# Mixture-of-experts stage on TensorE: the products with w1 and w3 run over a number of slot columns chosen per expert at run time

## The chip, the cores and the metric

The kernel runs on one core of a Trainium2 chip. The metric is the device time of one execution in microseconds. The kernel before took 5398.9 us (median of three runs, 5396.42 to 5399.67). All matrix products are in 32-bit floating point.

## The reference

Eight sequences of 512 tokens with 512 features each pass through three blocks, each followed by a residual sum and a layernorm: a Mamba block (state-space scan), a cross-attention block with 16 heads, and a mixture-of-experts block. Only the last one is touched by the change; cut to what matters it is

```
logits = x @ wg.T;  scores = softmax(logits)            # 4096 tokens, 32 experts
keep the 4 best of 8 groups, then the 4 best experts (K = 4); weights normalised over the 4
cap = int(1.25 * 4096 * 4 / 32)                         # 640 slots per expert
each (token, expert) pair takes the next free slot of that expert; pairs beyond 640 are dropped
xe  = tokens gathered by slot                           # 32 x 640 x 512, empty slots are zero
h   = silu(xe @ w1[e]) * (xe @ w3[e])                   # 512 x 512 weights per expert
out = (h @ w2[e]) * weight of the slot
y[token] += out;   plus a shared expert silu(x @ sw1) * (x @ sw3) @ sw2
```

Counted with the reference's own gate on its own inputs, the 32 experts receive between 316 and 750 pairs; 16025 of the 16384 pairs fit into the slots. One expert has at most 320 pairs, five have 321 to 384, six 385 to 448, five 449 to 512, six 513 to 576, and nine have more than 576.

## The kernel before

`layers` (line 89) computes Mamba, attention, the gate and the shared expert, interleaved by a hand-written order; it also writes each token's row, its weights and its number into a DRAM buffer `xbuf` that has 640 rows per expert. `experts` (line 1225 on) then walks the 32 experts in order, and `finish` (line 1472) does the last layernorm. A scheduler of the framework orders instructions within a stretch of straight code; the source order is its starting point, and each engine runs its own list strictly in order, with semaphore waits between engines.

For one expert `e`, `load(e + 1)` (line 1245) issues on SP's queue the next expert's token rows `xe` (L1250, 1362.5 KB) and its three weights `w` (L1253, 1024 KB each). `xe` has two buffers, so the load for expert e + 1 can only start when expert e - 1 no longer needs its own rows; their last readers are the five scatters of that expert (L1394), which take the row numbers from `xe`. `flip` (line 1279) transposes `xe` on TensorE, one slot tile of 128 rows at a time (five tiles, `CJ`), and DVE copies the result to `xT` (L1286). `sums_x` (line 1288) forms the sums that a Strassen-Winograd product needs: all 512x512 products are done as seven half-size products instead of eight, with the slots cut into two halves of 320 (`HALF`).

`hidden` (line 1319) is called twice per expert (r = 0, 1) and issues the seven products, each once for w1 and once for w3. `product` (line 1311) is two matmuls of 320 columns; each of them shows as two records in the profile. That makes 14 groups of eight records (one product for w1 and w3) per expert. ACT copies partial results out of PSUM (`keep`, L1328) and applies silu (L1341); DVE adds and multiplies (`use`, L1335 and L1339) into `hT`. The generator `side` lets DVE form weight sums for the next expert in between. `give` (line 1375) does the product with w2 for slot tiles 0 to 3 as seven half-size products of 256 columns, and slot tile 4 (the fifth, `j = CJ - 1`) as four plain matmuls of 512 columns (L1416, tile `po`), then scatters the five tiles of `y` with an accumulating indirect DMA on GpSimd (`put`, L1394). Between its steps it calls `between` (line 1447), which issues the five flips of the next expert.

All matmuls of all experts run at full width: 640 slots, filled or not. An empty slot holds zeros and a weight of zero.

## Time and profile before

| | |
|---|---|
| median of three runs | 5398.9 us |
| the profiled execution | 5406.3 us, of which the span of its instructions is 5404.6 us |
| TensorE (PE) busy | 4672.4 us, 86% |
| VectorE (DVE) busy | 4235.9 us, 78% |
| ScalarE (ACT) busy | 2593.6 us, 48% |
| one expert (4521.9 to 4569.8 us) | 47.9 us: PE 47.90, DVE 28.42, ACT 13.32, POOL 7.99 us busy |
| instruction fetches of PE (queue q8) | 137 packets of 16 KB |

The span is cut into 40 slices of 135 us. Layers fill the first 27 slices or so, with DVE busiest, and the experts the last 13, with PE busiest. In a group's row, "x" is the number of records and "mean ns" the length of one; matmul records overlap, so the distance between the starts of two runs of matmuls tells more than the mean of one. "PEld" is the loading of weights into the array, which overlaps the matmul before it. An arrow in the list of waits reads "engine, tile and line that waited <- what ended the wait: total, times, longest".

### The profile page before, as it was taken

Reading aid. Unit: us, or ns where it says so; the run is one execution under the profiler, and the core shown is the slowest. Engines: PE = TensorE matmul, PEld = TensorE weight load, DVE = VectorE, ACT = ScalarE, POOL = GpSimd, SP = SyncE. Lnnn points to the kernel's source line nnn. Section 1 sums busy time; section 2 is a strip of 40 time slices with the busy share of each in tenths; the row PEclk is TensorE's granted clock in tenths of the full one; section 3 lists DMA queues with packets and bytes.
Section 4 is the critical chain, followed back from the end, with each engine's and each line's share of the span. In section 5 each row is a group of like instructions: output and inputs, shape, how many; then the busy total and the mean of one; then the engine's idle time right before and its main releaser. Section 6 shows DMA issues by size and latency. Waiting matters only on the chain. (4 is left out here: it accounts for less than half of the span.)

```text
span 5404.6 us, 53991 instructions
## 1 busy us (share of the span) xinstructions
PE 4672.4 (86%) x17320; PEld 2476.6 (46%) x17320; DVE 4235.9 (78%) x5369; ACT 2593.6 (48%) x5726; POOL 570.3 (11%) x426
## 2 busy tenths in 40 slices
PE   6768889788888988988888888789999999999994
PEld 3324234234333423433333342333677777777773
DVE  7999899989989989898998998943566555665554
ACT  5566565565656556566565655523222222222223
POOL 1000002002000200200200020011111111111111
PEclk8879989999999999999999999899999999999997
DMA  8875346345444634634544463342344444544544
GB/s 236 266 224 146 87 96 208 81 114 176 114 104 117 197 77 109 189 98 107 174 125 100 117 200 78 91 146 66 103 128 127 123 117 118 127 127 121 129 115 144
DMA packets 486427, 719.03 MB, mean 133 GB/s; under 512 B 117137, under 2 KB 200625, under 8 KB 484096
## 3 DMA queue, kind: packets, MB, share of 16 engines
q1 hardware_dynamic: 450128, 627.16, 41.1%
q0 software_dynamic: 33280, 76.90, 7.5%
q10 hardware_dynamic: 2736, 11.54, 0.5%
q8 instruction: 137, 2.24, 0.2%
q14 instruction: 146, 1.20, 0.1%
HBM read 391.24 MB, written 165.05 MB: 103 GB/s over the span
## 5 line engine op out<-in xcount | busy, mean ns | idle before, releaser
L480 ACT ACTIVATE l_da<-rep,l_aneg 128x256 f32<-128x256 f32 x2048 | 895.0, 501 | 941.8 <-DVE h L501 877.0
L501 DVE TENSOR_TENSOR_SCAN h<-l_da,h 128x1028 f32<-128x1028 f32 x512 | 1166.0, 2292 | 20.3 <-ACT l_da L480 17.7
L494 DVE TENSOR_TENSOR h<-rep,bc 128x1024 f32<-128x1024 f32 x512 | 614.7, 1218 | 103.1 <-PE py L521 84.6
L510 DVE TENSOR_TENSOR h<-h,bc 128x1024 f32<-128x1024 f32 x512 | 619.5, 1217 | 2.1
L521 PE MATMUL py<-h,l_fold 128*32 128x512 f32 x2048 | 368.3, 644 | 113.4 <-DVE h L510 96.5
L813 PE MATMUL ps_s<-l_ka,l_qa 64*128 64x512 f32 x1024 | 325.6, 707 | 137.8 <-DVE mx L815 137.6
L1314 PE MATMUL ps_h<-xT,w 128*128 128x320 f32 x1536 | 435.8, 433 | 0.0
L1394 POOL DMA_INDIRECT based<-y,xe x160 | 255.5, 1597 | 1309.9 <-ACT y L1417 630.0
L1335 DVE TENSOR_TENSOR hT<-ps_h,p 128x320 f32<-128x320 f32 x128 | 62.9, 492 | 378.5 <-PE ps_h L1314 378.5
L815 DVE TENSOR_REDUCE mx<-ps_s 128x2 f32<-128x1024 f32 x256 | 310.2, 1217 | 58.5 <-PE ps_s L813 58.3
L1314 PEld LDWEIGHTS ps_h<-xT,w 128*128 128x128 f32 x1536 | 292.5, 191 | 118.3 <-issue 0.4
L855 PE MATMUL po<-eT,l_va 128*64 128x512 f32 x1024 | 301.5, 670 | 47.6 <-ACT eT L843 43.1
L839 PE MATMUL ps_t<-l_qa,l_ka 64*128 64x512 f32 x1024 | 308.4, 674 | 23.8 <-ACT eT L843 23.1
L843 ACT ACTIVATE eT<-ps_t 128x1024 f32<-128x1024 f32 x256 | 259.0, 1015 | 128.8 <-PE ps_t L839 128.5
L688 POOL DMA_INDIRECT xbuf<-x2t,dest x128 | 217.2, 1697 | 860.4 <-DVE dest L679 760.8
L1314 PE MATMUL ps_h<-t,s 128*128 128x320 f32 x1024 | 286.1, 432 | 0.0
L343 PE MATMUL ps_z<-xnT,wm 128*128 128x256 f32 x1024 | 238.0, 388 | 30.0 <-DVE o L561 24.3
L750 PE MATMUL ps_p<-x2T,wa 128*128 128x512 f32 x512 | 241.5, 626 | 18.1 <-ACT hT L944 10.4
L552 PE MATMUL po<-wm,zs 128*128 128x512 f32 x512 | 244.7, 632 | 13.8 <-DVE z L957 11.9
L343 PE MATMUL ps_x<-xnT,wm 128*128 128x256 f32 x1024 | 246.5, 393 | 4.5 <-ACT xnT L332 2.5
L343 PEld LDWEIGHTS ps_z<-xnT,wm 128*128 128x128 f32 x1024 | 194.6, 193 | 93.0 <-DVE o L561 37.5
L343 PEld LDWEIGHTS ps_x<-xnT,wm 128*128 128x128 f32 x1024 | 196.1, 195 | 80.5 <-issue 43.8
(232 smaller groups left out, 7170.4 us busy)
## 6 DMA issues: line engine op xcount, KB each, us to landing
w<-in_w SPq DMA_DIRECT2D x93, 1024.0 KB
wm<-in_in_proj_w SPq DMA_DIRECT2D x128, 512.0 KB
rep<-dt SPq DMA_DIRECT2D x256, 256.0 KB
rep<-dtx SPq DMA_DIRECT2D x256, 256.0 KB
xbuf<-zero SPq DMA_DIRECT2D x32, 1362.5 KB
xe<-xbuf SPq DMA_DIRECT2D x32, 1362.5 KB
wm<-in_out_proj_w SPq DMA_DIRECT2D x64, 512.0 KB
wa<-in_sw SPq DMA_DIRECT2D x24, 1024.0 KB
```

The source lines that it names most:

```text
L343: nc.tensor.matmul(ps[:, i, :], w[:, dc, i * P : (i + 1) * P], f["xnT"][:, dc, :], start=(dc == 0), stop=(dc == DC - 1),)
L480: nc.scalar.activation(da[:, n, 1:], dt[:, j, i, :], AF.Exp, scale=aneg[:, 2 * q + i, 2 * jj + j, g : g + 1])
L494: nc.vector.tensor_tensor(h[:, :, 1:], dtx.rearrange("p j i t -> p (j i) t"), f["bc", g][0], ALU.mult)
L501: nc.vector.tensor_tensor_scan(flat, da.rearrange("p n t -> p (n t)"), flat, 0.0, ALU.mult, ALU.add)
L510: nc.vector.tensor_tensor(h[:, :, 0:T], h[:, :, 1:], f["bc", g][1], ALU.mult)
L521: nc.tensor.matmul(f["py"][j * QP : (j + 1) * QP, :, :], fold, hs[j // 2][:, 2 * (j % 2) : 2 * (j % 2) + 2, 0:T], start=False, stop=g == N ...
L813: nc.tensor.matmul(ps[:, j, :], qa[r, lt * P : (lt + 1) * P], ka[r, :], start=True, stop=True)
L815: return lambda: nc.vector.tensor_reduce(mx[:, lt, :].unsqueeze(2), ps, AX.X, ALU.max) and None
L839: nc.tensor.matmul(ps[:, j, :], ka[r, kc * P : (kc + 1) * P], qa[r, :], start=True, stop=True)
L843: nc.scalar.activation(eT, ps, AF.Exp)
L855: nc.tensor.matmul(po[j * 2 * HD : (j + 1) * 2 * HD, :], va[:, kc, i, j * HD : (j + 2) * HD], eT[:, j, :], start=(kc == 0), stop=(kc == SC ...
L1314: nc.tensor.matmul(ps, w[:, n, r * P : (r + 1) * P], x[:, n, :], start=not more and n == 0, stop=n == 1, skip_group_check=more,)
```

## The change

The gate, after the last batch, computes for each expert a number from 0 to 5 into a new SBUF tile `arm`: how many of the thresholds 320, 384, 448, 512, 576 its number of pairs exceeds. It stands for the widths `COLS` = 160, 192, 224, 256, 288, 320 columns per half.

So that empty slots end up at the end of both halves, the halves are now the even and the odd slots: `flip`'s copy reads PSUM with a stride of two, and `use` writes `hT` with a stride of two.

At the start of each expert PE and DVE each load `arm[e]` into a register. Each of the seven steps of `hidden` becomes a `tc.Switch` on PE: six arms, one per width, each with the four matmuls (two of w1, two of w3) at that width; an indirect jump chooses the arm and each arm ends in a jump to the common exit. The other engines see no arms: ACT and DVE still work on all 320 columns, the columns beyond the width being stale. After each `hidden`, a Switch on DVE clears the columns of `hT` beyond the width. In `give`, slot tile 4 is a Switch too: the arms for up to 512 pairs are empty, the other two hold the four matmuls. PSUM tiles are now fixed rings, zeroed once, instead of pool tiles.

In the built program there are per expert 15 such jumps into an arm on PE (14 in `hidden`, one in `give`) and two on DVE. Each switch is a stride constant, two address instructions with the jump, and six arms; each arm begins with a prefetch hint for its own exit. The matmuls listed for PE grow from 9300 to 18388 and the branches from 2 to 2946. The position of the flips moves, too: before, the five flips of the next expert stood in `give`; in the changed program 16 of an expert's 20 transposes stand in the second `hidden`, the first of them after the 11th of its 14 switches.

```diff
+COLS = tuple(range(160, HALF + 1, 32))
+PE, DVE = mybir.EngineType.PE, mybir.EngineType.DVE
...
+        if not clock:
+            many, more = taken[:, SC, :], taken[:, 1, :]
+            nc.vector.tensor_scalar(more, many, float(2 * COLS[0]), None, ALU.is_gt)
+            for c in COLS[1:-1]:
+                to = arm if c == COLS[-2] else more
+                nc.vector.scalar_tensor_tensor(to, many, float(2 * c), more, ALU.is_gt, ALU.add)
...
-    psx = ctx.enter_context(tc.tile_pool(name="e_psx", bufs=3, space=PSUM))
-    psy = ctx.enter_context(tc.tile_pool(name="e_psy", bufs=2, space=PSUM))
+    psh = ctx.enter_context(tc.tile_pool(name="e_psh", bufs=1, space=PSUM))
...
+    def ring(n, width, name):
+        held = [psh.tile([P, width], F32, name=f"{name}{i}") for i in range(n)]
+        for t in held:
+            nc.vector.memset(t, 0.0)
+        return cycle(held)
+
+    xh, yh, oh = ring(3, HALF, "ps_x"), ring(2, HALF, "ps_y"), ring(2, D, "ps_o")
...
-        nc.vector.tensor_copy(got["xT"][:, :, j * P : (j + 1) * P], ps.rearrange("p (c t) -> p c t", c=DC))
+        to = got["xT"].rearrange("p c (k t) -> p c k t", k=2)[:, :, :, j * P // 2 : (j + 1) * P // 2]
+        nc.vector.tensor_copy(to, ps.rearrange("p (c t k) -> p c k t", c=DC, k=2))
...
-                ps, w[:, n, r * P : (r + 1) * P], x[:, n, :], start=not more and n == 0, stop=n == 1,
+                ps[:, 0:cols], w[:, n, r * P : (r + 1) * P], x[:, n, 0:cols], start=not more and n == 0, stop=n == 1,
...
-            to = hT[:, 2 * i + r, k * HALF : (k + 1) * HALF]
+            to = hT.rearrange("p c (t k) -> p c t k", k=2)[:, 2 * i + r, :, k]
...
+        def products(more, *parts):
+
+            for n in tc.Switch({PE: got["arm", PE]}, len(COLS)):
+                for ps, w, t in parts:
+                    product(ps, w, r, t, more, COLS[n])
...
-        for m, (w, s1, s2, s3, s4) in enumerate(ws):
-            product(xs[m], s2, r, t2, more=True)
-            pu.append(keep(xs[m], m, "pu"))
+        products(True, *((xs[m], ws[m][2], t2) for m in both))
+        pu = [keep(xs[m], m, "pu") for m in both]
...
+        for n in tc.Switch({DVE: got["arm", DVE]}, len(COLS)):
+            if COLS[n] < HALF:
+                nc.vector.memset(hT.rearrange("p (i r) t -> p i r t", r=2)[:, :, r, 2 * COLS[n] :], 0.0)
...
-        po = pso.tile([P, D], F32, tag="po", name="po")
-        for ic in range(DC):
-            nc.tensor.matmul(po, hT[:, ic, j * P : (j + 1) * P], w2[:, ic, :], start=(ic == 0), stop=(ic == DC - 1))
+        po = next(oh)
+        for n in tc.Switch({PE: got["arm", PE]}, len(COLS)):
+            for ic in range(DC if 2 * COLS[n] > j * P else 0):
+                nc.tensor.matmul(po, hT[:, ic, j * P : (j + 1) * P], w2[:, ic, :], start=(ic == 0), stop=(ic == DC - 1))
...
+        for engine, queue in ((PE, nc.tensor), (DVE, nc.vector)):
+            got["arm", engine] = queue.value_load(arm[0:1, e : e + 1])
```

More of the change, by code (lines that the diff above doesn't have):

```diff
@@ L1 @@
 from contextlib import ExitStack
-from itertools import chain
+from itertools import chain, cycle
 import concourse.bass as bass
@@ L86, in layernorm, with layers @@
     return wait(roots)
-def layers(ctx, tc, a, x1d, filld, based, xbuf):
+def layers(ctx, tc, a, x1d, filld, based, xbuf, arm):
     nc = tc.nc
@@ L1217, in layers, with experts @@
     dry()
-def experts(ctx, tc, a, xbuf, based):
+def experts(ctx, tc, a, xbuf, based, arm):
     nc = tc.nc
@@ L1235, in experts @@
     p2 = ctx.enter_context(tc.tile_pool(name="e_p2", bufs=2))
-    psx = ctx.enter_context(tc.tile_pool(name="e_psx", bufs=3, space=PSUM))
-    psy = ctx.enter_context(tc.tile_pool(name="e_psy", bufs=2, space=PSUM))
+    psh = ctx.enter_context(tc.tile_pool(name="e_psh", bufs=1, space=PSUM))
     pst = ctx.enter_context(tc.tile_pool(name="e_pst", bufs=1, space=PSUM))
-    pso = ctx.enter_context(tc.tile_pool(name="e_pso", bufs=2, space=PSUM))
+    def ring(n, width, name):
[4 more added lines that the diff above has]
+    xh, yh, oh = ring(3, HALF, "ps_x"), ring(2, HALF, "ps_y"), ring(2, D, "ps_o")
     ident = cp.tile([P, P], F32, name="e_ident")
@@ L1309, in sums_w2, with product @@
             yield
-    def product(ps, w, r, x, more=False):
+    def product(ps, w, r, x, more=False, cols=None):
         for n in range(2):
             nc.tensor.matmul(
-                ps, w[:, n, r * P : (r + 1) * P], x[:, n, :], start=not more and n == 0, stop=n == 1,
+                ps[:, 0:cols], w[:, n, r * P : (r + 1) * P], x[:, n, 0:cols], start=not more and n == 0, stop=n == 1,
                 skip_group_check=more,
@@ L1341, in use @@
                 nc.scalar.activation(to, v, AF.Silu)
-        p1, pu, p5 = [], [], []
-        xs = [None, None]
-        for m, (w, s1, s2, s3, s4) in enumerate(ws):
-            xs[m] = psx.tile([P, HALF], F32, tag="h", name="ps_h")
-            product(xs[m], A(w, 0, 0), r, B(x, 0, 0))
-            p1.append(keep(xs[m], m, "p1"))
-        for m, (w, s1, s2, s3, s4) in enumerate(ws):
-            ps = psy.tile([P, HALF], F32, tag="h2", name="ps_h")
-            product(ps, A(w, 0, 1), r, B(x, 1, 0))
-            use(m, 0, 0, ps, p1[m])
+        def products(more, *parts):
+            for n in tc.Switch({PE: got["arm", PE]}, len(COLS)):
+                for ps, w, t in parts:
+                    product(ps, w, r, t, more, COLS[n])
@@ L1353, in hidden @@
+        xs = [next(xh) for m in both]
+        products(False, *((xs[m], A(ws[m][0], 0, 0), B(x, 0, 0)) for m in both))
+        p1 = [keep(xs[m], m, "p1") for m in both]
+        ys = [next(yh) for m in both]
+        products(False, *((ys[m], A(ws[m][0], 0, 1), B(x, 1, 0)) for m in both))
+        for m in both:
+            use(m, 0, 0, ys[m], p1[m])
         next(side, None)
-        for m, (w, s1, s2, s3, s4) in enumerate(ws):
-            product(xs[m], s2, r, t2, more=True)
-            pu.append(keep(xs[m], m, "pu"))
+        products(True, *((xs[m], ws[m][2], t2) for m in both))
@@ L1357, in hidden @@
+        pu = [keep(xs[m], m, "pu") for m in both]
         next(side, None)
-        ys = []
-        for m, (w, s1, s2, s3, s4) in enumerate(ws):
-            ys.append(psy.tile([P, HALF], F32, tag="h2", name="ps_h"))
-            product(ys[m], s1, r, t1)
-            p5.append(keep(ys[m], m, "p5"))
+        ys = [next(yh) for m in both]
+        products(False, *((ys[m], ws[m][1], t1) for m in both))
+        p5 = [keep(ys[m], m, "p5") for m in both]
         next(side, None)
-        for m, (w, s1, s2, s3, s4) in enumerate(ws):
-            product(xs[m], s3, r, t3, more=True)
+        products(True, *((xs[m], ws[m][3], t3) for m in both))
@@ L1366, in hidden @@
+        for m in both:
             use(m, 1, 1, xs[m], p5[m])
-        for m, (w, s1, s2, s3, s4) in enumerate(ws):
-            product(ys[m], s4, r, B(x, 1, 1), more=True)
+        products(True, *((ys[m], ws[m][4], B(x, 1, 1)) for m in both))
+        for m in both:
             use(m, 0, 1, ys[m], pu[m])
         next(side, None)
-        for m, (w, s1, s2, s3, s4) in enumerate(ws):
-            product(xs[m], A(w, 1, 1), r, t4, more=True)
+        products(True, *((xs[m], A(ws[m][0], 1, 1), t4) for m in both))
@@ L1373, in hidden @@
+        for m in both:
             use(m, 1, 0, xs[m])
+        for n in tc.Switch({DVE: got["arm", DVE]}, len(COLS)):
+            if COLS[n] < HALF:
+                nc.vector.memset(hT.rearrange("p (i r) t -> p i r t", r=2)[:, :, r, 2 * COLS[n] :], 0.0)
     def give(e, got, side):
@@ L1408, in give @@
         for r in both:
-            xs.append(psx.tile([P, HALF], F32, tag="h", name="ps_o")[:, 0:FH])
+            xs.append(next(xh)[:, 0:FH])
             product(xs[r], A(hT, 0, 0), r, BW(w2, 0, 0))
@@ L1420, in give @@
         for r in both:
-            ps = psy.tile([P, HALF], F32, tag="h2", name="ps_o")[:, 0:FH]
+            ps = next(yh)[:, 0:FH]
             product(ps, A(hT, 0, 1), r, BW(w2, 1, 0))
@@ L1429, in give @@
         for r in both:
-            zs.append(psy.tile([P, HALF], F32, tag="h2", name="ps_o")[:, 0:FH])
+            zs.append(next(yh)[:, 0:FH])
             product(zs[r], s1, r, t1)
@@ L1518, in program @@
     nc = tc.nc
-    with tc.tile_pool(name="dram", bufs=1, space=DRAM) as dram:
+    with tc.tile_pool(name="dram", bufs=1, space=DRAM) as dram, tc.tile_pool(name="one", bufs=1) as one:
         x1d = dram.tile([N, D], F32, name="x1d")
@@ L1524, in program @@
         xbuf = dram.tile([SLOTS, ROW], F32, name="xbuf")
+        arm = one.tile([P, E], I32, name="arm")
         nc.scalar.preload_act_table_set(LN_EXP)
         with ExitStack() as ctx:
-            layers(ctx, tc, a, x1d, filld, based, xbuf)
+            layers(ctx, tc, a, x1d, filld, based, xbuf, arm)
         with ExitStack() as ctx:
-            experts(ctx, tc, a, xbuf, based)
+            experts(ctx, tc, a, xbuf, based, arm)
         with ExitStack() as ctx:
```

## The prediction

> **What bounds the kernel now.** I read the page's busy row and slices first, to see which stage the change is in and who is busy there.

> ```profile
> PE 4672.4 (86%) x17320; PEld 2476.6 (46%) x17320; DVE 4235.9 (78%) x5369; ACT 2593.6 (48%) x5726; POOL 570.3 (11%) x426
> ...
> PE   6768889788888988988888888789999999999994
> ...
> DVE  7999899989989989898998998943566555665554
> ...
> PEclk8879989999999999999999999899999999999997
> ...
> q8 instruction: 137, 2.24, 0.2%
> ```

> The last 13 slices are the experts: PE full, DVE about half. Next the windows of one expert, from the first product of its `hidden` to that of the next, and of the tail.

> ```profile
> 4521.90:4569.80 47.90, 47.90 (x198) 35.43 (x197) 28.42 (x52) 13.32 (x29) 7.99 (x5) 1.00 0.49 122
> 5300.00:5404.60 104.60, 34.01 (x133) 24.89 (x131) 41.26 (x137) 36.76 (x70) 9.25 (x6) 0.68 0.53 178
> ```

> PE is busy 47.90 of 47.90 us at a granted clock of 1.00; DVE 28.42. So an expert lasts as long as its matmuls. The timeline of PE gives their price by distance of starts:

> ```profile
> 4499.86 2.32 PE L1314 MATMUL ps_h<-xT,s 128*128 128x320 f32 x8
> 4502.01 2.32 PE L1314 MATMUL ps_h<-t,w 128*128 128x320 f32 x8
> 4504.16 0.60 PE L1285 MATMUL ps_t<-e_ident,xe 128*128 128x128 f32 x4
> 4504.60 1.89 PE L1314 MATMUL ps_o<-w,hT 128*128 128x256 f32 x8
> 4506.33 3.60 PE L1416 MATMUL po<-w,hT 128*128 128x512 f32 x8
> 4509.76 0.60 PE L1285 MATMUL ps_t<-e_ident,xe 128*128 128x128 f32 x4
> ```

> Eight records of 320 columns take 2.15 us, of 256 columns 1.73, of 512 columns 3.43, four of 128 columns 0.44: 0.84 ns per column each. An expert is 14 x 2.15 + 7 x 1.73 + 3.43 + 5 x 0.44 = 47.8 us.

> Last, the scatters and the load that follows them (POOL's timeline, then SP's), because `xe` is loaded only when they are done:

> ```profile
> 4520.16 1.54 POOL L1394 DMA_INDIRECT based<-y,xe  x1 [7.49 <-DVE y L1391]
> 4527.77 1.54 POOL L1394 DMA_INDIRECT based<-y,xe  x1 [6.07 <-DVE hT L1339]
> 4533.32 1.54 POOL L1394 DMA_INDIRECT based<-y,xe  x1 [4.01 <-ACT hT L1341]
> 4538.85 1.54 POOL L1394 DMA_INDIRECT based<-y,xe  x1 [3.98 <-ACT p L1328]
> ```
> ```profile
> 4543.50 0.37 SPq L1250 DMA_DIRECT2D xe<-xbuf  x1
> 4551.14 0.37 SPq L1253 DMA_DIRECT2D w<-in_w  x1
> ```

> The scatters follow each other at 5.5 us; the load starts 4.65 us after the last, and the DMA view of that stretch shows its bytes until 4549.2. That is 27.3 us after this `hidden` began (4521.9); the first transposes come at 4552.0. The slack is 2.8 us.

> **What the change removes.** With the counts per expert, mean width is (160 + 5x192 + 6x224 + 5x256 + 6x288 + 9x320)/32 = 261 columns of 320. `hidden` drops from 30.1 to 24.6 us of matmuls per expert, 177 us over 32. Seventeen experts leave out `po`, 17 x 3.43 = 58 us. Together 236 us of PE, 4.4%, if nothing takes its place. Divided by 480 jumps that is 0.49 us per jump.

> **What it adds on PE's sequencer.** 480 switches, each with a jump in and a jump out. The trace of before has no jump inside the work, so I bound it. Near end: at the start of the program's timeline POOL goes through a branch and starts again 0.29 us later; with code already there a switch is 0.6 us of sequencer time, and PE has 1.76 us of matmuls per switch to hide it. Far end: code that must be fetched. q8 shows how PE gets code: 137 packets of 16 KB for 34,640 records and 611 semaphore instructions, one per 257, the last at 5299.7 us with 270 records to go, so code is fetched about one packet ahead of what runs. Windows of 5 us that hold one such packet give it 1.5% and 1.3% of 16 engines, 1.2 and 1.0 us. The first load of the kernel is issued at 0.81 us and its first bytes appear in the DMA view at 1.9: 1.1 us. So a fetch on demand is 1.1 + 1.2 = 2.3 us; between 1.2 (the packet alone) and 3.75 us (that first load, 0.81 to its user at 4.56).

> Do the arms have to be fetched? Packed together, six arms are some 108 instructions and lie inside the next packet. Against that: the dispatch multiplies an index by a stride constant, and every arm begins with a hint to prefetch its own exit. A hint for a jump of 18 instructions would serve nothing, so I take each arm and each exit to lie in another fetch unit. The jump in has no hint. Then a switch is: fetch of the arm 2.3, waiting first for the packet ahead that the sequencer started on its own (1.2), fetch of the exit 2.3 (hinted, but the arm's instructions are too few to cover it), two jumps 0.6: T = 6.4 us. Bounds: 2 x 1.2 + 0.6 = 3.0 and 2 x 3.75 + 1.2 + 0.6 = 9.3. As T is above the 1.76 us of matmuls, PE runs dry in each.

> [...]

> **The sum per expert.** `hidden`: 14 x 6.4 = 89.6 us; 16 of the 20 transposes lie inside its stalls and add nothing. `give`: seven products 12.1, four transposes 0.4, `po` 3.43 x 15/32 = 1.6, and its jump, of which the group of 1.7 us ahead covers a part: 4.7. Loading `arm` into PE's register has no row: between 0.3 (a jump) and 3.75 (a load), taken 2.0, since the queue is short there. DVE's switch at the end of the second `hidden` stands before `sums_w(got, "hT")` and the first product of `give` reads what it clears: 6.4 plus a clear of up to 640 columns (0.8, from DVE's 128x640 rows), less PE's own exit fetch 2.3 and 0.9 of transposes: 4.0 (1 to 7). In sum 114.4 us against 47.9, +66.5, times 32 = +2128. The profiled execution took 5406.3 us, 7.4 above the median: 5406.3 + 2128 - 7.4 = 7527, said as 7500.

> **Edits costed at nothing, and their cover.** Copies and `use` with stride two: 5 x 0.69 and 12 x 0.49 us per expert; even doubled, DVE has 28.4 + 9.3 of 47.9 us, and more now. ACT still copies full width, 13.3 us. DVE's switch after the first `hidden`, 6.4 us, delays `use` of the next steps, which PE reaches 6.4 us apart. Gate: five small DVE operations (0.17 us each), off the path of the scatters. Seven clears of PSUM (about 0.5 us each) lie beside the first `xe` load, for which PE waited 10.6 us. Jumps on ACT, POOL and SP between blocks, 16 x 0.3 = 4.7 us per expert, lie beside idle time. PE idle half the time may lower its clock (0.68 in the tail against 1.00), under stalls too.

> **The rivals.**
> (1) The arms are near and a jump costs under a microsecond; this decides below T = (30.1 + 1.8)/14 = 2.3 us. For it: 108 instructions. Against: the hints. PE would have 40.5 us per expert, but the moved transposes meet `xe`: it lands 27.3 us after `hidden` begins, the transposes now stand after 11 products, 11 x 1.76 = 19 us. PE waits, then 3 x 1.76 + 2.2 + 13.7: 48.4 us, about what it was. So 5415 us if the scatters keep their pace, down to 5399 - 236 = 5163 if they do not hold it up. This is the one that ends on the other side.
> (2) One fetch per switch: the hint works, or the arms are near and exits far. T = 2.3 + 1.2 + 0.3 = 3.8; 53.2 + 14.1 + 2.1 + 4 = 73.4, +25.5 x 32 = +816: 6210.
> (3) Fetches are slower than a single one looks, T of 8 to 9.3: 140 to 162 us per expert: 8340 to 9060.
> (4) The registers hold 5 throughout and nothing is shortened: in my case no visible difference in time, as PE waits for code anyway; the widths of the records would tell.

> **Chances.** Rival 1: 0.10, half of it faster and half within 0.2% (about what a measurement of this kernel can tell from no change) or a trifle above. Rival 2: 0.20. Forecast, T of 5 to 8 (6820 to 8340): 0.55. Rival 3: 0.15. Faster 0.05, same 0.04, slower 0.91. The range leaves out rival 1 and a third of rival 3: from 5770, which is T = 3.0 (42 + 14.1 + 1.3 + 2 = 59.4, +368), to 8900.

> **What the profile would show.** Right: records at L1329 in groups of eight, idle time of several us between them on PE with no semaphore as releaser; q8 packets up from 137 to over 1000; PE's share in the experts near 40%; period about 114 us; `po` in 15 experts; DVE, ACT and POOL waiting for PE. Wrong: groups back to back, or PE waiting for `xe` at the transposes (rival 1); an exit without a gap after the arm (rival 2). I am wrong most easily in whether arms lie in separate fetch units, and in the length of one fetch under the experts' own DMA traffic (share 0.49).

## The result and the profile after

The changed kernel takes 8929.3 us (median of four runs, 8926.91 to 8945.81); the kernel before took 5399.3 us beside it. The ratio is 1.654, with a 95% interval of 1.650 to 1.657. The direction of the forecast was right, and so was its cause, jumps whose code has to be fetched; the size was not: 7500 us was forecast, 8900 us was the upper end. The profiled execution has a span of 8944.1 us.

The page of the changed kernel, the lines that answer to those shown of before: busy time of the engines, two of the rows of 40 slices (tenths busy, tenths of full clock), and the queue that brings instructions.

```profile
PE 5476.8 (61%) x17184; PEld 2932.2 (33%) x17184; DVE 4239.1 (47%) x5427; ACT 2586.0 (29%) x5726; POOL 581.5 (7%) x426
...
PE   6788888888888887854434443443544545345442
...
PEclk8899999999999999866565656665666767567655
...
q8 instruction: 1860, 30.47, 2.0%
```

The first 17 slices, everything ahead of the experts, look as they did. From there on PE is busy three to five tenths of the time and runs at a granted clock of five to seven tenths; before it was full at full clock. Packets of instructions went from 137 to 1860. The windows view of the experts alone gives the clock as 0.64 and the DMA share as 0.18 (one expert before: 1.00 and 0.49):

```profile
3600.00:8800.00 5200.00, 2474.21 (x6612) 1629.27 (x6610) 957.70 (x1772) 472.48 (x986) 274.19 (x171) 0.64 0.18 43
```

The list of what PE waited for from 3400 to 8900 us (total, times, longest, in us) names no semaphore for nine tenths of it. "issue" is time in which the engine waited for nothing that the profile shows:

```profile
PE ps_x L1329 <- issue: 1315.6, 283, 10.2
PE ps_y L1329 <- issue: 1088.7, 186, 11.0
...
PE ps_o L1435 <- issue: 67.7, 15, 8.3
PE ps_x L1329 <- DVE hT L1354: 51.0, 20, 3.7
PE ps_y L1329 <- DVE t L1323: 45.0, 23, 2.4
...
PE ps_y L1329 <- DVEq L1389: 12.3, 3, 4.5
```

L1329 is the product inside the switches; `ps_o` waits 15 times, once for each expert that has its fifth tile. The timeline of PE shows one group of eight per switch and the gap ahead of it (brackets: idle time before):

```profile
6066.16 2.92 PE L1329 MATMUL ps_x<-t,s 128*128 128x192 f32 x8 [9.01 <-issue]
6077.91 2.92 PE L1329 MATMUL ps_y<-t,s 128*128 128x192 f32 x8 [8.84 <-issue]
6087.49 2.92 PE L1329 MATMUL ps_x<-xT,w 128*128 128x192 f32 x8 [6.65 <-issue]
```

The gaps are 7 to 9 us, and the 8 records of 192 columns take 2.92 us at the lower clock (granted 0.50 from 6066.0 to 6069.1 us; it would be 1.29 us at the 0.84 ns per column of before). Where the gaps are spent, PE's own sequencer says. These are the instructions of the line that holds all jumps, and of the line that loads the arm index (minimum, median and maximum in ns; "q" marks an engine's sequencer):

```profile
L1582 PEldq COMPARE_BRANCH  x1024: 181/4610/8945, 3795.2 to 8856.4; - x171
...
L1582 DVEq COMPARE_BRANCH  x608: 41/41/69, 3795.5 to 8854.0; - x152
```
```profile
L1487 PEldq TENSOR_LOAD <-arm x32: 302/307/496, 3794.3 to 8704.2; - x32
```

The median jump on PE is 4.61 us. 960 of its 1024 jumps take over 2 us, 4398 us together; 4398/32 = 137 us of the 158.4 us between one expert's register load and the next (47.9 us before). Laid beside the instruction packets, jump by jump, nearly all of the 960 show the same course: a pause, one packet (228 jumps, median 3.3 us in all) or two that overlap (731 jumps, 4.75 us), and a second pause. In the medians of the jumps with two packets it is 0.53 us until the first packet starts, 2.57 us until the later one ends, and 1.6 us until the jump ends (1.4 us with one packet). A packet takes 0.98 us where it came alone and 1.76 us where two came; ahead of the experts it took 1.01 us. The DMA view of 6057 to 6069.5 us, in which two jumps start, has four packets in 3.9% of the time of 16 engines, 7.8 us:

```profile
q8 instruction: 4, 0.07, 3.9%
```

The price also depends on where a jump lands. The median jump in and out, by expert: 4.4 to 4.7 and 4.6 to 5.0 us for arms 1 to 4; 2.9 and 4.8 us for the one expert with arm 0, whose code comes next behind the jump; 4.5 to 4.9 and 2.9 to 3.2 us for arm 5, whose exit comes next in line. These cheaper jumps are those with one packet: 13 of the 15 into arm 0 and 134 of the 135 out of arm 5. So experts with arms 0 and 5 lasted 141.3 and, in the mean, 142.3 us, the others 165 to 168 in the mean, wide or narrow.

### The profile page after: what moved, and what is told of

The parts are those of the page before. It is cut to its first block, busy times and chain, and to the rows that moved or that the text cites. A ratio compares the mean times of both kernels' runs of the same rounds, so it can differ in the third digit from the quotient of the medians.

```text
span 8944.1 us, 59172 instructions
## 1 busy us (share of the span) xinstructions
PE 5476.8 (61%) x17184; PEld 2932.2 (33%) x17184; DVE 4239.1 (47%) x5427; ACT 2586.0 (29%) x5726; POOL 581.5 (7%) x426
## 5 line engine op out<-in xcount | busy, mean ns | idle before, releaser
L1329 PE MATMUL ps_x<-xT,w 128*128 128x320 f32 (+5 forms) x1024 | 478.3, 647 | 602.9 <-issue 602.9
L1301 DVE COPY xT<-ps_t 128x512 f32<-128x512 f32 x160 | 110.1, 688 | 1087.2 <-PE ps_t L1299 1086.3
L1329 PE MATMUL ps_y<-t,s 128*128 128x256 f32 (+5 forms) x768 | 307.2, 565 | 419.0 <-issue 418.3
L1329 PEld LDWEIGHTS ps_x<-xT,w 128*128 128x128 f32 x1024 | 315.1, 326 | 753.2 <-issue 715.0
L1329 PE MATMUL ps_x<-t,s 128*128 128x256 f32 (+5 forms) x768 | 310.0, 574 | 327.7 <-issue 324.4
L1329 PE MATMUL ps_y<-xT,s 128*128 128x320 f32 (+5 forms) x512 | 237.9, 645 | 336.0 <-issue 336.0
L1329 PE MATMUL ps_x<-t,w 128*128 128x320 f32 (+5 forms) x512 | 235.2, 638 | 277.9 <-issue 250.5
L1329 PEld LDWEIGHTS ps_y<-t,s 128*128 128x128 f32 x768 | 208.7, 286 | 512.9 <-issue 482.1
L1329 PE MATMUL ps_y<-xT,w 128*128 128x320 f32 (+5 forms) x512 | 205.5, 571 | 246.5 <-issue 181.7
L1329 PEld LDWEIGHTS ps_x<-t,s 128*128 128x128 f32 x768 | 213.6, 292 | 412.6 <-issue 380.3
```

The lines of the kernel that those rows point to most:

```text
L1301: nc.vector.tensor_copy(to, ps.rearrange("p (c t k) -> p c k t", c=DC, k=2))
L1329: nc.tensor.matmul(ps[:, 0:cols], w[:, n, r * P : (r + 1) * P], x[:, n, 0:cols], start=not more and n == 0, stop=n == 1, skip_group_check= ...
```

## The experiments

All times below stand against runs of the kernel before on the same chip (5404 to 5407 us). Kernels that share an edit are told together.

### The change without its jumps

```diff
-        for engine, queue in ((PE, nc.tensor), (DVE, nc.vector)):
-            got["arm", engine] = queue.value_load(arm[0:1, e : e + 1])
+        for engine in (PE, DVE):
+            got["arm", engine] = ARMS[e]
```

> The changed kernel with the arm of each expert taken from a table in the program (the arms that these inputs give) in place of registers and jumps; widths, rings, layout and the clearing of the unused columns stay. It leaves out the choice at run time, so it is valid for these inputs' counts only. Theory A (the whole loss is jumps on TensorE): the 8929 us fall below the kernel before; arms 0 to 3 are held by the load of the expert's tokens at about 41.5 us per expert, arm 4 by 45 and arm 5 by 47.8 us, so 5399 - 124 = about 5275 us, and 5163 us if that load does not bind. Theory B (reading every second column, the fixed rings of PSUM tiles or the clearing cost time of their own): 5400 us or more, with TensorE idle on VectorE or PSUM tiles. Theory C (the lower granted clock of the changed kernel's experts, 0.64 against 1.00, is a cause and not a consequence): the clock stays below 0.8 in the experts, and the time is above 5600 us.

Measured: 5363.7 us, ratio 0.992 (0.991 to 0.994). Theory A holds for the loss: without the jumps (and the register loads and VectorE's switches that go with them) all 3530 us are gone, the clock in the experts is back at 0.95, and so theory C falls; theory B, which asked for 5400 us or more, falls with it. But of the 124 us expected only 42 came. The list of PE's waits in the experts says why (there was no such wait before):

```profile
PE ps_t L1300 <- DMA xe<-xbuf: 153.7, 22, 15.1
```

Experts that could last 35 to 45 us last about 46, because the scatters, the load of `xe` and the transposes come round once in that time. My floor of 41.5 us had left out that a shorter expert hardly brings the last scatter forward. In a narrow expert of this program the first scatter, that of the empty slot tile, comes early, at 22 us after `hidden` began, but the second comes at 43 to 46 us and the last at 62 to 66, and the load 5 us later; in the kernel before it was 46 and 65. These four scatters follow the products with w2, and those follow the transposes that wait for the load.

### Full width in every arm, jumps kept

```diff
-                    product(ps, w, r, t, more, COLS[n])
+                    product(ps, w, r, t, more, WIDE[n])
```

> The changed kernel with every arm of the product switches at the full 320 columns; the jumps, the empty slot tile left out and the clearing stay. Theory A (jumps set the period, the matmuls between two jumps only add to it): every expert comes to the period of the widest arm or a little more; the product work that comes back is 177 us at full clock, some 270 us at the granted 0.64, so 9100 to 9200 us; should fetches run beside the matmuls, 8930 us. Rival (short arms are themselves the trouble, because a fetch ahead has too little work to hide behind): with more work in each arm the exit jump gets shorter, and the time stays at 8930 us or falls.

Measured: 9204.1 us, ratio 1.703 (1.700 to 1.706), 275 us above the changed kernel. The jumps are as they were:

```profile
L1583 PEldq COMPARE_BRANCH  x1024: 181/4612/8118, 3811.5 to 9124.1; - x171
```

So the rival falls: more work in an arm shortens no jump. The number agrees with theory A's 9100 to 9200, but by luck. Wider matmuls run beside the jumps: from one jump into an arm to the next it is 8.3 to 11.1 us in the mean in 13 of the 14 steps of `hidden`, as in the changed kernel (8.7 to 11.3). Only the ninth step grew, from 9.7 to 18.2 us. There the scheduler has now put 420 of the 640 weight loads of the transposes, which in the changed kernel stand spread over the steps from the eleventh on, and so the transposes wait 209 us longer for VectorE's copies (241.4 against 32.5 us).

### Two arms in place of six

```diff
-COLS = tuple(range(160, HALF + 1, 32))
+COLS = (256, HALF)
```

> The changed kernel with two widths (256 and 320) in place of six, so that one arm lies next behind the jump and the other next ahead of the exit. Theory A1 (a jump costs 4.7 us when it lands beyond the code that comes next in line, and 3.1 to 3.4 us when it lands on the next stretch, as arm 0's way in and arm 5's way out did): one of the two jumps of each switch becomes cheap, about 1.4 us less on 480 switches, some 670 us less: 8200 to 8350 us, experts at about 142 us. Rival A2 (the price is the same wherever the jump lands, and arms 0 and 5 were cheaper by their other work): 8900 us. Rival A3 (the number of arms sets the price, as the table of six is walked through): 7000 us or less.

Measured: 8542.4 us, ratio 1.580 (1.577 to 1.583).

```profile
L1578 PEldq COMPARE_BRANCH  x1024: 181/3502/8016, 3803.3 to 8446.5; - x171
```

The median jump falls from 4.61 to 3.50 us and the sum of all jumps from 4411 to 3801 us, 610 less, near the 670 expected (A1); the time falls by 387 us only and misses the 8200 to 8350 us, as the transposes wait 145 us longer for VectorE (177.7 against 32.5). They stand in fewer steps here, too: the ninth grew from 9.7 to 15.2 us. A2 and A3 fall: where a jump lands sets its price, and the number of arms does not.

### A compare-and-branch over code in line

```diff
-            for n in tc.Switch({PE: got["arm", PE]}, len(COLS)):
-                for ps, w, t in parts:
-                    product(ps, w, r, t, more, COLS[n])
+            with tc.If(got["arm"] == 0) as cmp:
+                for ps, w, t in parts:
+                    product(ps, w, r, t, more, COLS[0])
+            with cmp.Else():
+                for ps, w, t in parts:
+                    product(ps, w, r, t, more, COLS[1])
```

> Two widths (256 and 320), chosen by one compare-and-branch over code that stands in line without gaps: the 16 instructions of the narrow arm, a jump over the 16 of the wide one. VectorE's clearing switch is gone (the unused columns hold finite values of an earlier expert, in slots that carry weight 0). Theory A (a jump is dear because its target is not among the instructions already fetched, and is cheap where it is): a jump costs 0.2 to 0.5 us, 480 of them 100 to 240 us; 17 of 32 experts save 9.5 us each, 161 us: 5300 to 5480 us, with some 200 instruction packets in place of 1860. Rival (every taken jump on TensorE empties its fetch and costs about 4.7 us wherever it lands): one taken jump per switch, 480 x 4.7 = 2256 us: 7500 us or more.

Slot tile 4 is chosen in the same way, and VectorE's switches are gone. Measured: 5909.0 us, ratio 1.094 (1.092 to 1.096): 430 us more than theory A, 1600 less than the rival. The price of a jump follows theory A, and hardly any jump shows as a wait on the products (5.9 us, at the jump of slot tile 4):

```profile
q8 instruction: 170, 2.79, 0.2%
```
```profile
PE ps_t L1295 <- DMA xe<-xbuf: 357.9, 29, 14.5
PE ps_t L1295 <- DVE xT L1297: 67.5, 86, 0.8
PE ps_x L1325 <- ACT p L1339: 26.7, 29, 1.2
```

The first fence is from the page, the second the list of PE's waits in the experts. Of 735 recorded jumps the median takes 0.18 us and the longest 0.46, and they run ahead of the queued matmuls: there is no "issue" wait. The time went into waits, most of them for the load of `xe`. In PE's list of instructions the transposes now begin after eight or nine of the 14 groups of `hidden`, where the scheduler had put them; in the kernel before they begin with `give`, five or six groups (11 to 13 us) later. A wait cost more than its own length here: the first matmuls behind one ran slower (8 records of 320 columns at 4577.1 us, behind a wait of 10.4 us, took 4.38 us, others 2.32), and the clock in the experts is 0.89 where it was 1.00. PE was busy there for 1523 us, although the narrower products save 161 us of the 1515 of before.

### A third buffer for xe

```diff
-        got["x"] = xe = p2.tile([P, CJ, ROW], F32, tag="xe", name="xe")
+        got["x"] = xe = p2.tile([P, CJ, ROW], F32, tag="xe", name="xe", bufs=3)
```

Made in four programs: the one with the branch and two widths, the one with the table, one with all six widths, and the kernel before.

> The program with one compare-and-branch and two widths, and a third buffer for the expert's tokens (xe). Theory A (there the jumps cost nothing visible, and the 510 us over the kernel before were the loop of five scatters, the load of xe into the buffer that they free, and the transposes, which in that program stand ahead of the products): with the load one expert earlier the loop is gone, TensorE binds again, and 17 narrow experts save 9.5 us each: 5399 - 161 = 5240 us, up to 5360 if the recorded 117 us of jumps show in full. Rival B (the wait on xe only stood where the cost of the branches would have been): 5700 us or more, idle time on TensorE with no releaser or with VectorE.

> The program with the arms from a table (valid for these inputs' counts only) and a third buffer for xe. Theory A (its 5364 us, in place of the 5275 expected, came from the loop of scatters and xe load, which holds every expert to 45 to 48 us): with the third buffer each expert falls to its product time, 5399 - 177 - 58 = 5164 us, at most 5200. Rival (VectorE or the PSUM tiles in fixed rings hold it): 5300 us or more.

> The kernel before with nothing but the third xe buffer. Theory A (before, TensorE never waited for xe, the load landed just in time): no change, 5404 us, within 0.2%. Rival (the buffer alone is worth something, and the gains of the programs with it are partly its own): 5350 us or less.

Measured: with the branch 5735.9 us (ratio 1.061, 1.060 to 1.063), with the table 5271.5 us (0.976, 0.974 to 0.977), the kernel before 5403.7 us (0.9995, 0.9986 to 1.0005).

The kernel before gains nothing: its load of `xe` held nothing up, as read in the forecast. With the table the wait for `xe` is gone, and what is left in PE's list of waits is

```profile
PE ps_t L1300 <- DVE xT L1302: 66.4, 24, 7.8
```

VectorE in turn waited 102 us, in 32 waits, for the weights (22.6 us in the kernel before), so the load of 3 MB per expert is the likely next limit, which I did not test by itself; the expected 5164 us was missed by 107. With the branch, neither theory fits: the number is rival B's, but 333.7 us of waits for `xe` remained. With a third buffer the scheduler moved the transposes earlier still: in PE's list the first slot tile of an expert is transposed in the `hidden` of the expert two before it, and the rest follows in `give` and in the next `hidden`. So the first one waits for a load that has only just been issued: one issued at 4588.59 us held the transposes until 4594.91.

### Six widths in line, and a jump that is made long

The first has the six widths of the change, chosen by nested tests (an arm less than `mid`, else the rest). The second has, in 64 of 480 choices, a third arm (36 times the products) that never runs and lies between the two others:

```diff
+                    with tc.If(got["arm"] == 2) as cmp2:
+                        some(2)
+                    with cmp2.Else():
+                        some(1)
```

> All six widths, chosen by nested compare-and-branch over code in line (two or three tests, jumps of up to 10 KB of instructions, six arms of 2 KB), and the third xe buffer; no clearing by VectorE. Theory near (a jump is cheap as long as its target lies in the stretch of code already fetched or next in line; one packet of instructions is 16 KB, so most jumps here stay inside): the full narrowing, 5164 us, and up to 200 us of jumps: 5165 to 5370 us, some 300 to 480 packets of instructions. Rival (every jump beyond a few instructions is dear): two dear jumps per choice, 8000 us or more. Between them (jumps that cross into the next 16 KB wait for a packet of 1 us): 5500 to 6200 us.

> The program with one compare-and-branch, two widths and the third xe buffer, and in 64 of its 480 choices (the first of each half of an expert) a third arm that is never taken: 36 times the products, 72 KB of instructions, which lies between the two others and has to be jumped over. Theory A (the price of a jump is the distance: a target whose instructions are not fetched): one far jump in each of these 64 choices, 4.7 us each less up to 2 us that TensorE's queue of products covers, +170 to +300 us over the same program without that arm, with 64 to 190 more packets of instructions. Rival B (the price was the switch's own way of jumping, to a computed target): within 30 us of that program.

(An arm is 16 instructions, and one packet of 16 KB served some 256 of them, so an arm is 1 KB and not the 2 KB of these texts: six arms are 6 KB, the arm never taken is 36 KB.)

Measured: six widths 5572.9 us (ratio 1.031, 1.029 to 1.033), a time of the middle case foreseen, but not for its reason: 226.1 us are waits for `xe`, and the products wait 10.5 us with no releaser. The long jump: 5852.5 us (1.083, 1.081 to 1.084), 117 us above the same program without that arm. In narrow experts the program with the long jump differs from its neighbour in nothing but the distance to the exit, in wide ones in one more test, too. This is what its jumps take at the line of the added test (30 = 15 wide experts, two times each):

```profile
L1366 PEldq COMPARE_BRANCH  x30: 3323/4924/8188, 3803.3 to 5599.9; - x30
```

All its jumps take 454 us in place of 119; 335/64 = 5.2 us in the mean for each far one, like a jump of the switch, and packets rise from 170 to 294, about two per far jump. So distance alone brings the price, without a computed target; nor have the exits of the switch a computed target (the address instructions stand ahead of the entries alone), and they cost as much as its entries. How far apart the arms of a switch lie no view shows. Whether its jumps are dear by distance as well, or because they drop code that had been fetched, the runs do not separate. Only 117 of these 335 us show in the time, less than the 170 expected. The waits without a releaser grew by 156 us, the rest of the jumps ran beside queued matmuls; the waits for `xe` fell by 147 us (from 333.7 to 186.5), and PE was busy 82 us longer with the same matmuls (1550 against 1469 in the experts), so they ran slower.

### The transposes back in their place

```diff
-        for r in range(2):
-            hidden(got, r, sums_w2(got) if r == 0 else sums_w(nxt, "w1") if nxt else iter(()))
-        give(e, got, between(nxt) if nxt else iter(()))
+        with tc.manual_schedule(engines={PE}):
+            for r in range(2):
+                hidden(got, r, sums_w2(got) if r == 0 else sums_w(nxt, "w1") if nxt else iter(()))
+            give(e, got, between(nxt) if nxt else iter(()))
```

In the texts that follow, "the same" is the program of the second one, with three widths.

> The same with two widths (256 and 320). Theory A: 17 experts save 9.5 us each, 5404 - 161 = 5243 us, up to 5290 where jumps show. Rival B: 5500 us or more.

> Three widths (224, 256, 320) by nested compare-and-branch in line, the third xe buffer, and TensorE's instructions of the experts kept in the order in which they are written, so that the transposes of the next expert's tokens stand in its second half again. Theory A (what held the earlier programs with these branches above 5570 us was the place of the transposes, which the scheduler had put one expert early, where the load of xe had just been issued): no wait on xe, jumps hidden behind the queued products; 12 experts at 224 and 5 at 256 columns save 139 us, the empty fifth tile 58 us: 5404 - 197 = 5207 us, and up to 5300 where the load of the weights or the jumps show, as in the program without jumps (5271). Rival B (the branches themselves hold the experts): 5500 us or more.

> The same with all six widths, up to 12 KB of code per choice. Theory A: 5404 - 235 = 5169 us, no better than the 5271 us of the program with the arms from a table (which waits for the load of the weights), and the recorded jumps of up to 2.2 us, some 40 to 80 us: 5270 to 5350 us, so no gain over three widths. Rival B: 5500 us or more, as in the program whose transposes stood early.

Measured: two widths 5272.3 us (ratio 0.9745, 0.9728 to 0.9761), three 5270.8 us (0.9749, 0.9732 to 0.9765), six 5288.2 us (0.9777, 0.9763 to 0.9792). These are faster than the kernel before by 2.2 to 2.6%. Against the same program without the order, two widths fall from 5735.9 to 5272.3 us: 464 us. The edit fixes the order of all of PE's instructions in the experts. That the gain comes from the transposes is read from the waits: those for `xe` (333.7 us) are gone, those for VectorE's copies fall from 49.4 to 10.0, and without the stops the same matmuls take 1382 us of PE in place of 1469. The timeline of PE with two widths, from the end of one expert (records of 256 columns) into the next, which is a wide one; PE's waits in the whole of the experts; and the windows view of them:

```profile
4567.76 1.89 PE L1325 MATMUL ps_y<-w,s 128*128 128x256 f32 x8
4569.49 0.60 PE L1295 MATMUL ps_t<-e_ident,xe 128*128 128x128 f32 x4
4569.92 1.89 PE L1325 MATMUL ps_x<-t,hT 128*128 128x256 f32 x8
4571.65 2.32 PE L1325 MATMUL ps_x<-xT,w 128*128 128x320 f32 x8
4573.81 2.32 PE L1325 MATMUL ps_y<-xT,w 128*128 128x320 f32 x8
```
```profile
PE ps_t L1295 <- DVE xT L1297: 10.0, 11, 2.0
PE ps_t L1295 <- DVE s L1286: 7.4, 16, 0.6
```
```profile
3800.00:5200.00 1400.00, 1381.28 (x6115) 1101.81 (x6114) 865.27 (x1608) 420.65 (x927) 259.73 (x157) 1.00 0.50 127
```

Groups follow each other by 2.15 us although a branch stands between them, PE waits 19 us in all, and the clock is 1.00. An undisturbed wide expert takes 47.86 us, as before, a narrow one 39.13, where the narrower products and the missing fifth tile save 14 x 0.43 + 3.43 = 9.45 and 38.4 would be expected: at most 0.7 us show for its jumps. Six widths bring nothing more: the groups that wait at their jumps are few,

```profile
PE ps_y L1329 <- issue: 12.0, 9, 2.2
```

with 13 jumps over 2 us of 1631, and the waits of transposes for VectorE come back (42.1 us), as in the program without jumps. All three times lie in the ranges expected, but the times that the saved matmuls alone would give, 5243, 5207 and 5169 us, were not reached. With two widths PE itself is the limit (busy 1381 of 1400 us in the view above). With three and six it is busy 1356 and 1324 us and waits for the copies of VectorE, which in turn waits 49 and 56 us for the weights (14 us with two widths). This points to the load of the weights, as in the program without jumps, and was not tested.

## Why the prediction was right or wrong

**Bound, and what the change removes: right in kind.** PE bound the experts, and idle PE without a releaser is what the change brought. The 236 us removed were real work, but not all of it could be had: without jumps 42 us came, with the third buffer 133 (5404 - 5271). The slack of 2.8 us between the load of `xe` and the transposes, read from the scatters, was the right warning; rival 1 had used it.

**Whether each arm and each exit has to be fetched: right.** Of the 960 dear jumps 959 brought one or two packets. The long jump in the program with plain branches shows that distance alone does it. Inside the changed kernel even the jumps to the code next in line (2.9 and 3.1 us) brought one packet, the others mostly two. The forecast's reason, arms in fetch units of their own, was not seen directly.

**The hint: right.** It runs about 0.1 us ahead of the exit jump, and no gain from it shows: the exits, which have it, took 4.68 us in the median, the dear entries 4.55.

**The length of a fetch on demand: wrong, and this is the failed step.** It was summed as 1.1 us to the first bytes and 1.2 us for the packet, 2.3 in all, with 3.75 as its bound. The median jump took 4.61 us, beyond that bound. Three things were missing: after the last packet another 1.4 to 1.6 us pass before the sequencer goes on; in most jumps two packets come, not one; and as they overlap, each takes 1.76 us in place of 1.0. The start, 0.53 us, was shorter than taken. The "packet ahead" of 1.2 us, which I had set ahead of the entry alone, may be the second of the two packets; it is paid at the exit as well.

**The sum with the measured size.** Two jumps of 4.6 us and some 0.6 us around them make T = 9.8 in place of 6.4, and the trace has 137.5/14 = 9.8 us from one switch of `hidden` to the next. The sum is then 14 x 9.8 + 12.1 + 0.4 + 1.6 + (9.8 - 1.7) + 0.3 + 4.0 = 163.7 us per expert, against 158.4 measured: the part behind the 14 switches was taken as 26.5 us and took 20.9. So T lies above the 9.3 that was the upper bound of the forecast and of rival 3 (T of 8 to 9.3, 8340 to 9060 us, chance 0.15). That 8929 us fell among the times of rival 3 all the same is luck: the smaller part made up for it. The range ended at 8900 and left out the top of rival 3, 160 of 720 us and not the third that the forecast says. The row that would have pointed there was the 3.75 us from the first load's issue to its user: for these fetches, too, what counted is when the user ran, 1.4 to 1.6 us after the last packet, not when the bytes moved.

**The small terms.** Loading the register was taken as 2.0 us between 0.3 and 3.75; it took 0.31. The 0.3 us of a jump was read from a pause of 0.29 us on POOL, in which the trace has a drain and semaphores but no branch; near jumps on PE took 0.17 to 0.18 us in the median. The switch on VectorE was taken as 4.0 us per expert; PE's waits for `hT`, `t` and VectorE's sequencer come to 51.0 + 45.0 + 16.4 + 12.3 = 125 us, 3.9 per expert, if all of them are put down to it. The lower clock was named, and does not bind: matmuls ran while the exit was being fetched (the exit jump at 6066.18 us took 6.67 us, the eight matmuls beside it were over after 2.9), and even full width in every arm left the steps of `hidden` without transposes as long as they were (8.3 to 11.1 us against 8.7 to 11.3).

**The signs.** Groups of eight with gaps of several us, over 1000 packets and `po` in 15 experts came as described. PE's share in the experts was 48% in place of 40, since slower matmuls count as busy; the period was 158 us in place of 114.

## What to carry to other kernels

Before a choice at run time is put on a busy engine, ask where its targets lie in the instruction stream: 480 choices cost 3530 us where each arm had to be fetched, and at most 0.7 us per expert where two arms stood in line within a few KB. A gain on the engine that binds is worth only the slack of the loop beside it, so look for that loop first (here scatters, load, transposes: 42 of 236 us came until it was opened). And when control flow is put into a scheduled program, read where the scheduler has moved the work around it: leaving TensorE's instructions, five transposes per expert above all, in their written order was worth 464 us.

## What was not expected

The granted clock of TensorE fell to 0.64 in the experts of the changed kernel and came back to 1.00 with the gaps gone, so it followed the idle time. A packet of instructions took 1.0 us alone and 1.8 us when two were under way, although the DMA share was 0.18 in place of 0.49; in the program with the long jumps, where mostly one came while a jump waited, it was 1.04 us, so two at once seem to slow each other. And one unused stretch of 36 KB between two arms brought back the full price of a far jump, 5.2 us.
